# Moving a linear term, the eviction of a unit and the last group's PSUM banks in a woven four-layer kernel

## The chip, the cores and the metric

The kernel runs on one core of a Trainium2 chip, as one program in one launch. The metric is the device time of that core in microseconds (us); the runs of the kernel before have a median of 7454.95 us (three runs, 7451.15 to 7469.55). A core has a matrix engine (TensorE, PE in the profile; its weight loads are listed as PEld), VectorE (DVE), ScalarE (ACT), GpSimd (POOL) and SyncE (SP), which issues nearly all DMAs here. Each engine takes its own instructions strictly in order and waits for the others by semaphores. Matmuls write to PSUM, which has eight banks of 128 x 512 float32.

## The reference

The input is 16 images of 32 channels and 128 x 128 points, float32. Four layers follow, each added to its own input after a group normalisation `_gn`:

```python
x = x + _L0_conv_ref(_gn(x), ...)   # recurrent layer over 128 columns
x = x + _L1_conv_ref(_gn(x), ...)   # sum of absolute differences, 3x3
x = x + _L2_conv_ref(_gn(x), ...)   # 2-d Hartley transform, 32x32 modes mixed
x = x + _L3_conv_ref(_gn(x), ...)   # edge operators, small U-net, product
```

The second layer is the costly one. Input and weights are rounded to whole numbers of up to 127, and each output is

```python
out = -jnp.sum(jnp.abs(patches[None] - w[:, None]), axis=1)   # 32 channels x 9 taps
```

for 32 output channels, which no matrix product computes. The kernel uses |x - w| = 2 max(x - w, 0) - (x - w): the sum of max(x - w, 0) needs one element-wise pass per weight, the sum of x is a convolution with equal weights (the *linear term*), the sum of w is a constant. The fourth layer normalises the image, applies five fixed edge operators normalised over channels and rows, conv1 to conv4 with pooling, three transposed convolutions with conv5 to conv7, and multiplies its normalised input with the result.

## The kernel before, in words

**Stage 0** (`stage0`) is the recurrent layer. It isn't touched.

**The difference stage** (`Differences.run`, L608) walks over 16 images in two halves of 64 rows: 32 *units*. `q` holds one half, four copies of its 32 channels over the 128 partitions, one for each of four output channels that are computed at once. For each of 72 steps `i` (8 sets of four output channels x 9 taps) one pass writes max(q - w, 0) into a tile of 128 x 64 x 128 half-precision values: on DVE (L681, `d_dve`, three buffers) or on ACT (L678, `d_act`, two buffers). `sums` (L579) then adds the tile up over channels with 16 matmuls (L584) into the unit's four PSUM banks `acc1`. `linear` (L592, L600) adds the linear term, 9 taps x 16 matmuls; here it stands first, and its first tap has `start=True`, which clears the banks. `finish` (L563) evicts the unit before: four `scalar_tensor_tensor` (L567) from PSUM into the residual `xr`, then four `bn_stats` (L569). The four banks are used by one unit after the other, so nothing of the new unit can be summed before the old one is evicted. In the kernel before, `finish` is issued when three `d_dve` tiles of the new unit stand unsummed (L640), then comes the whole linear term, then the sums.

**The background.** The other two layers run in four *groups* of four images (`After.work`, L887): `forward` (transform, `mixing`), `back` (inverse transform and residual), `statistics` of the edge operators (L1263), `conv1`, `small_layers`, `last`. A group may start once its four images have left the difference stage; groups 0, 1 and 2 are one generator and follow each other. It is woven into the difference stage by a planner, `Weave` (L300), when the program is built. The planner keeps estimated times for PE, DVE and ACT. The background is a generator: a positive yield is PE time just issued, a negative one a time to let pass before the next step, `SUMMED` a wait for PE. `advance` (L384) lets steps out while PE is free ahead of the next sum. So the yields and the `weave.dve += ...` entries decide only where an instruction stands in its engine's order; they are no waits on the chip. `keep_order` fixes that order. The background has four PSUM banks (`b_ps`), the difference stage the other four.

**The drain** (`drain`, L403). After the last unit two generators run alternately by their planned times: what is left of groups 0 to 2 (`weave`), and group 3 (`end.weave`), which takes over the four banks of the difference stage (`c_ps`).

Places that the change touches in the background:

- `mixing` (L1082): 32 steps of 16 small matmuls; the weights come in eight tiles `mix` of 1 MB, in a ring of three. A new one is loaded once a tile has been used.
- `back` (L1117): 16 steps; `take_out` (L1171) adds two PSUM banks to the residual (L1176) and takes statistics (L1178). At the end `normalised` leaves mean and scale in `stats3`.
- `frames` (L1217): loads padded images of x3 and scales them on ACT (L1248); its first call makes `fr_shift` on DVE (L1245).
- `spread` (L1532): adds a bias and writes a layer's output on the engine it is told.
- `last` (L1659): four units of two rounds. A round sums conv7 into four banks (`up.round`, L808), then for each of four images `s` = bank x scale + 1 (L1730) and `multiply` (L1692): two strided `scalar_tensor_tensor` (L1695) of 256 values a partition. `done` (L1701) adds the mean on ACT (L1703), `store` writes 2 MB in four DMAs (L1709), `reload` loads the unit after next (L1673). A DMA covers 8 rows of all 32 channels of four images: 32 partitions, four runs of 4 KB each. The x1 tiles of the difference stage (`jc_rows`, L294: four row blocks x 32 channels over 128 partitions, one run of 4 KB each) have the other arrangement.

Of the kernel before, what the change touches and what calls it, by code (L numbers as in the profile page):

```python
# [299 lines left out]
class Weave:  # L300
# [10 lines left out]
    def __init__(self, work):  # L311
# [3 lines left out]
        self.draining = False  # L315
# [87 lines left out]
def drain(*weaves):  # L403
# [4 lines left out]
    while live:  # L408
        w = min(live, key=lambda w: w.now)
        us = w.step()  # L410
        w.now = max(w.now + (us or 0.0), w.until)
        w.due(float("inf") if us is None else w.now)
        if us is None:
            live.remove(w)

# [22 lines left out]
def rest(nc, tc, cst, sel16, bias, m1, r1, a, d, out):  # L438


    with ExitStack() as ctx:
# [13 lines left out]
        end.side, end.ps = "right", ctx.enter_context(tc.tile_pool(name="c_ps", bufs=4, space=PSUM))  # L455
        end.weave = Weave(end.work([NG - 1]))
# [5 lines left out]
class Differences:  # L462
# [100 lines left out]
    def finish(self, b, half, acc, xr):  # L563
# [4 lines left out]
        for k in range(4):  # L568
            nc.vector.bn_stats(self.stat[:, b, 4 * half + k, :], v[k])  # L569
        def store():  # L570
# [5 lines left out]
        self.weave.dve = max(self.weave.dve, self.weave.pe) + 5.6  # L576
        self.weave.later(max(self.weave.dve - self.weave.base, 0.0) + 0.5, store)

    def sums(self, acc, d, i, last):  # L579
        c = 1 if i % 3 == 1 else 0  # L580
        for k in range(4):
            for j in range(4):
# [5 lines left out]
                    start=False,  # L588
# [3 lines left out]
    def linear(self, acc, q):  # L592

        for tap in range(9):
            kh, kw = tap // 3, tap % 3
            for j in range(4):
                for k in range(4):
                    rows = slice(32 * k, 32 * k + 32)
                    row = 16 * j + 4 * k + kh
                    self.nc.tensor.matmul(  # L600
                        acc[k][32 * j : 32 * j + 32, :],
                        self.sel16[rows, 8, :],
                        q[rows, row : row + 4, kw : kw + W],
                        start=tap == 0,
                        stop=False,
                    )

    def run(self, tc, ctx, weave):  # L608
# [16 lines left out]
        for b in range(B):  # L625
            for half in range(2):
                q, acc = following, None
                late, xq = [], {}

                def sums(until, last):  # L630

                    while late and (min(late)[0] <= until or last):
                        end, n, act, t = min(late)
                        late.remove((end, n, act, t))
                        self.sums(acc, t, n, last and not late)
# [3 lines left out]
                for i in range(72):  # L639
                    if not acc and sum(not v[2] for v in late) == 3:  # L640

                        if before:
                            self.finish(*before)
                            weave.pe = max(weave.pe, weave.dve)
                        acc = [ps.tile([128, 512], F32, name="acc1") for _ in range(4)]
                        self.linear(acc, q)
                        weave.pe += 4.0
                        sums(weave.dve, False)
                    if i == 8 and (b, half) != (B - 1, 1):
# [38 lines left out]
                    else:  # L688
                        weave.advance(weave.dve + (3 - made) * DVE_US + (5.6 if before else 0.0))
# [1219 lines left out]
```

## Time and profile before

| what | value |
|---|---|
| runs, median of 3 | 7454.95 us (7451.15 to 7469.55) |
| profiled execution | 7434.2 us |
| its span, first to last instruction | 7432.4 us |
| mean granted TensorE clock | 0.86 |
| busy: PE / DVE / ACT | 5602.5 / 5881.6 / 5276.7 us |
| difference taps on ACT (L678) | 593 x 7146 ns |
| difference taps on DVE (L681) | 1711 x 2361 ns |
| linear term on PE (L600) | 4608 matmuls, 151.8 us |
| evictions (L567) | 128 x 745 ns |
| DMA | 721.68 MB, 31% of 16 engines' time |

A row of groups has the line, engine, operation and tile, the count, busy time and mean duration. A row of waits has the instruction that waited, what released it, the sum, the number of times and the longest. In a timeline each row is start, length, engine, line, operation, tile; the bracket holds the idle time of the engine before it and what ended it. In a table by stretches the numbers after the length are busy times of PE, PE weight load, DVE, ACT and POOL with counts, then the clock, the DMA share and GB/s. In the chain of waits PE has 14% of the span by steps that the trace can follow, most of it in the drain.

### The profile page before, as it was taken

How to read it: one execution, taken by the hardware profiler on the slowest of the kernel's cores; microseconds unless marked ns; L12 is line 12 of the kernel's file. 1: busy time of each engine (PE TensorE's matmuls, PEld its weight loads, DVE VectorE, ACT ScalarE, POOL GpSimd, SP SyncE). 2: the span in 40 equal slices, each digit the busy share in tenths (PEclk: the TensorE clock that was granted, in tenths of full speed). 3: DMA queues.
4: the chain of work that ended last, by engine and by line, in shares of the span. 5: the costliest groups of instructions: out<-in, count | busy, mean ns of one | idle time of the engine just before them, and what ended most of it. 6: DMA issues, size and time to landing. Idle time of an engine off the chain costs nothing. (4 is left out here: it accounts for less than half of the span.)

```text
span 7432.4 us, 258307 instructions
## 1 busy us (share of the span) xinstructions
PE 5602.5 (75%) x121132; PEld 3087.2 (42%) x121132; DVE 5881.6 (79%) x7180; ACT 5276.7 (71%) x3110; POOL 34.2 (0%) x31
## 2 busy tenths in 40 slices
PE   4888466666676777998777676998777775898897
PEld 3666232222244343333344343333335345554554
DVE  7787599999988989999898988998898994135223
ACT  2556398889987988898898888898887980122222
POOL 0000000000000000000000000000000000000000
PEclk9899788888878888999888887998888885897996
DMA  8655111111033333111433332221343234244314
GB/s 314 225 183 172 61 64 54 46 53 52 33 95 95 119 110 96 57 53 46 98 108 103 102 111 94 63 67 42 75 113 108 82 117 144 65 141 119 80 30 95
DMA packets 374270, 721.68 MB, mean 97 GB/s; under 512 B 50896, under 2 KB 219856, under 8 KB 362320
## 3 DMA queue, kind: packets, MB, share of 16 engines
q1 hardware_dynamic: 372768, 704.58, 31.0%
q8 instruction: 948, 15.53, 0.9%
q14 instruction: 122, 1.00, 0.0%
q10 hardware_dynamic: 432, 0.57, 0.0%
HBM read 507.21 MB, written 164.32 MB: 90 GB/s over the span
## 5 line engine op out<-in xcount | busy, mean ns | idle before, releaser
L678 ACT ACTIVATE d_act<-q,neg 128x8192 f16<-128x8192 f16 (+1 forms) x593 | 4199.2, 7146 | 559.1 <-PE acc L584 512.6
L681 DVE TENSOR_SCALAR d_dve<-q,qw 128x8192 f16<-128x8192 f16 (+1 forms) x1711 | 3941.9, 2361 | 348.3 <-PE acc L584 306.1
L584 PE MATMUL acc<-d_dve,sel 128*32 128x512 f16 x27376 | 1963.3, 416 | 747.7 <-DVE d_dve L681 734.5
L584 PEld LDWEIGHTS <-sel 128*32 128x32 f16 x36864 | 1078.8, 103 | 2405.6 <-issue 1816.9
L1603 PE MATMUL acc<-xp,wf 32*32 32x512 f32 x25600 | 1014.7, 620 | 30.6 <-issue 15.2
L584 PE MATMUL acc<-d_act,sel 128*32 128x512 f16 x9488 | 738.6, 438 | 256.1 <-ACT d_act L678 244.0
L1603 PEld LDWEIGHTS acc<-xp,wf 32*32 32x32 f32 x25600 | 443.5, 105 | 404.4 <-issue 299.4
L1542 ACT ACTIVATE y<-pooled,b 32x128 f32<-32x128 f32 x512 | 204.7, 400 | 519.2 <-DVE pooled L1528 510.4
L819 PE MATMUL acc<-y,u_conv 32*32 32x256 f32 (+1 forms) x9728 | 443.3, 515 | 87.4 <-DVE s L1730 39.5
L207 PE MATMUL pg<-h,wb 64*64 64x20 f32 (+15 forms) x4096 | 403.1, 324 | 95.3 <-DVE h L256 54.1
L207 PE MATMUL pg<-e,wb 64*64 64x20 f32 (+15 forms) x4096 | 360.4, 320 | 16.0 <-DVE e L260 4.3
L244 ACT ACTIVATE gt<-pg,bias 128x20 f32<-128x20 f32 (+15 forms) x1024 | 315.5, 374 | 78.1 <-PE pg L207 70.9
L1248 ACT ACTIVATE xp<-xp,fr_shift,stats 128x1280 f32<-128x1280 f32 (+1 forms) x128 | 182.8, 1434 | 230.1 <-DMA xp<-x_d 174.2
L207 PEld LDWEIGHTS pg<-h,wb 64*64 64x64 f32 x4096 | 251.1, 156 | 131.0 <-DVE h L256 80.7
L819 PEld LDWEIGHTS acc<-y,u_conv 32*32 32x32 f32 x9728 | 199.7, 119 | 252.0 <-issue 155.4
L207 PE MATMUL pg<-xn,wb 64*64 64x28 f32 (+61 forms) x4096 | 291.1, 308 | 10.7 <-ACT gt L244 3.3
L207 PEld LDWEIGHTS pg<-e,wb 64*64 64x64 f32 x4096 | 256.1, 158 | 94.0 <-DVE e L260 65.8
L600 PE MATMUL acc<-q,sel 32*32 32x512 f16 x4608 | 151.8, 532 | 148.1 <-DVE xr L567 99.1
L1703 ACT ACTIVATE xr<-xr,l_ms 128x1024 f32<-128x1024 f32 x64 | 69.9, 1140 | 267.1 <-DVE xr L1695 267.1
L255 ACT ACTIVATE th<-c 128x20 f32<-128x20 f32 (+15 forms) x256 | 81.3, 320 | 239.7 <-DVE c L253 238.2
L1288 PE MATMUL acc<-xp 32*64 32x204 f32 (+3 forms) x8576 | 233.2, 343 | 13.5 <-issue 13.5
L207 PEld LDWEIGHTS pg<-xn,wb 64*64 64x64 f32 x4096 | 222.5, 157 | 35.7 <-ACT gt L244 8.3
(203 smaller groups left out, 4215.5 us busy)
## 6 DMA issues: line engine op xcount, KB each, us to landing
xr<-x_d SPq DMA_DIRECT2D x192, 512.0 KB
xp<-x_d SPq DMA_DIRECT2D x112, 640.0 KB
q<-q_d SPq DMA_DIRECT2D x32, 2145.0 KB
x_d<-xr SPq DMA_DIRECT2D x128, 512.0 KB
x_in<-in_x_dram SPq DMA_DIRECT2D x16, 2048.0 KB
res<-in_x_dram SPq DMA_DIRECT2D x64, 512.0 KB
xn<-in_xs_dram SPq DMA_DIRECT2D x64, 512.0 KB
xn<-xn SPq DMA_DIRECT2D x128, 256.0 KB
```

Source lines behind the costliest of these rows:

```text
L207: nc.tensor.matmul(bank[c][q][64 * pair : 64 * pair + 64, :, :width], wb[half, 4 * kind + KIND[q]].rearrange("p b o -> p (b o)"), v[half], ...
L244: nc.scalar.activation(gt[:, q, :, :n], bank[c][q][:, :, :n], AF.Tanh if q == G else AF.Sigmoid, bias=bias[:, KIND[q] : KIND[q] + 1],)
L255: nc.scalar.activation(th[:, :, :n], cell, AF.Tanh)
L584: self.nc.tensor.matmul(acc[k][32 * j : 32 * j + 32, :], self.sel16[:, i // 9, :], d[:, row : row + 4, c : c + W], start=False, stop=last,)
L600: self.nc.tensor.matmul(acc[k][32 * j : 32 * j + 32, :], self.sel16[rows, 8, :], q[rows, row : row + 4, kw : kw + W], start=tap == 0, stop ...
L678: nc.scalar.activation(dst, src, AF.Relu, bias=self.neg[:, i : i + 1])
L681: nc.vector.tensor_scalar(dst, src, self.qw[:, i : i + 1], 0.0, ALU.subtract, ALU.max)
L819: nc.tensor.matmul(acc[blk][32 * j : 32 * j + 32, o : o + rows * n], t[part, 4 * par + tap, :], src[part, top : top + rows, left : left + ...
L1248: nc.scalar.activation(v, v, AF.Identity, bias=shift[0], scale=self.stats3[:, 1])
L1288: nc.tensor.matmul(gram[blk][j : j + width, at : at + n], xp[part, l, 2 + j : 2 + j + width], xp[part, rows, j : j + width + 4], start=sta ...
L1542: nc.scalar.activation(d, s, AF.Identity, bias=bj)
L1603: nc.tensor.matmul(acc[blk][32 * j : 32 * j + 32, :], tap_of("all", tap)[rows], xp[rows, 4 * j + kh : 4 * j + kh + 4, kw : kw + W], start= ...
```

## The change

The linear term no longer stands first. `linear` does one tap a call, called at every fourth step from 24 to 56; none of its matmuls starts the banks, and the first sum of a unit has `start=True` instead. The eviction is issued at two unsummed `d_dve` tiles, not three, and the planner counts 2.6 us for it before PE may go on, 5.6 for DVE.

In the background: `mixing` has places in its order for the weights (five of 5 us), `take_out` stands 4.5 instead of 7 us after its step, the shift of the frames is made at the end of `back`. In `last` the DMAs take one image each over all 128 partitions, `s` is written with its two column phases interleaved, and `multiply` is one contiguous instruction. When one of the drain's generators has ended, the other is `alone`: its `acc` takes banks from both pools by turns of four, `spread` uses DVE for even and ACT for odd images, and a store is planned 4 instead of 14 us after its unit.

```diff
 def drain(*weaves):
...
         if us is None:
             live.remove(w)
+            for w in live:
+                w.alone = True
...
         end.side, end.ps = "right", ctx.enter_context(tc.tile_pool(name="c_ps", bufs=4, space=PSUM))
+        end.spare = bg
...
-        self.weave.dve = max(self.weave.dve, self.weave.pe) + 5.6
+        start = max(self.weave.dve, self.weave.pe)
+        self.weave.pe, self.weave.dve = start + 2.6, start + 5.6
...
-    def sums(self, acc, d, i, last):
+    def sums(self, acc, d, i, first, last):
...
-                    start=False,
+                    start=first,
                     stop=last,
...
-    def linear(self, acc, q):
+    def linear(self, acc, q, tap):
-        for tap in range(9):
-            kh, kw = tap // 3, tap % 3
-            for j in range(4):
+        kh, kw = tap // 3, tap % 3
+        for j in range(4):
...
-                        start=tap == 0,
-                        stop=False,
+                    start=False,
+                    stop=False,
+        self.weave.pe = max(self.weave.pe, self.weave.now) + 0.45
...
-                        self.sums(acc, t, n, last and not late)
+                        self.sums(acc, t, n, not summed, last and not late)
+                        summed += 1
...
-                    if not acc and sum(not v[2] for v in late) == 3:
+                    if not acc and sum(not v[2] for v in late) == 2:
                         if before:
                             self.finish(*before)
-                            weave.pe = max(weave.pe, weave.dve)
                         acc = [ps.tile([128, 512], F32, name="acc1") for _ in range(4)]
-                        self.linear(acc, q)
-                        weave.pe += 4.0
                         sums(weave.dve, False)
+                    if i % 4 == 0 and 24 <= i < 60:
+                        self.linear(acc, q, i // 4 - 6)
...
-                        weave.advance(weave.dve + (3 - made) * DVE_US + (5.6 if before else 0.0))
+                        weave.advance(weave.dve + (2 - made) * DVE_US + (2.6 if before else 0.0))
...
     def acc(self):
-        return self.ps.tile([128, 512], F32, name="acc")
+        self.banks += 1
+        ps = self.spare if self.weave.alone and self.banks // 4 % 2 else self.ps
+        return ps.tile([128, 512], F32, name="acc")
...
-            yield 1.1
+            yield 1.0
+            if ky % 4 == 3 and 8 < ky < M1 - 1:
+                yield -5.0
...
                 if previous:
-                    yield -7.0
+                    yield -4.5
                     take_out(*previous)
...
             yield from normalised(nc, zp_, self.ps, weave, mv, 1, cst["avg2_bc"], 1e-5, self.stats3)
+            nc.vector.scalar_tensor_tensor(
+                self.shift3, self.stats3[:, 0], -1.0, self.stats3[:, 1], ALU.mult, ALU.mult
+            )
+            yield -2.5
...
-                if not shift:
-                    shift.append(pool.tile([128, 1], F32, name="fr_shift"))
-                    nc.vector.scalar_tensor_tensor(
-                        shift[0], self.stats3[:, 0], -1.0, self.stats3[:, 1], ALU.mult, ALU.mult
-                    )
-                nc.scalar.activation(v, v, AF.Identity, bias=shift[0], scale=self.stats3[:, 1])
+                nc.scalar.activation(v, v, AF.Identity, bias=self.shift3, scale=self.stats3[:, 1])
...
-            if engine is nc.vector:
+            if blk % 2 == 0 if weave.alone else engine is nc.vector:
...
-            def at(t, unit, j):
-                first = t.offset + g * 4 * CHW + (32 * unit + 8 * j) * W
-                return bass.AP(t.tensor, first, [[HW, 32], [CHW, 4], [1, 8 * W]])
+            def at(t, unit, blk):
+                first = t.offset + (4 * g + blk) * CHW + 32 * unit * W
+                return bass.AP(t.tensor, first, [[8 * W, 4], [HW, 32], [1, 8 * W]])
...
-                for j in range(4):
-                    nc.sync.dma_start(xr[32 * j : 32 * j + 32], at(self.d["x3"], unit, j))
+                for blk in range(4):
+                    nc.sync.dma_start(xr[:, blk], at(self.d["x3"], unit, blk))
...
-                for pc in range(2):
-                    v = x[:, blk].rearrange("p (r a w b) -> p r a w b", a=2, b=2, w=64)[:, :, pr, :, pc]
-                    nc.vector.scalar_tensor_tensor(v, v, mean[:, blk : blk + 1], s[:, pc], ALU.subtract, ALU.mult)
-                weave.dve += 1.0
+                v = x[:, blk].rearrange("p (r a w) -> p a r w", a=2, w=W)[:, pr]
+                nc.vector.scalar_tensor_tensor(
+                    v, v, mean[:, blk : blk + 1], s.rearrange("p r w b -> p r (w b)"), ALU.subtract, ALU.mult
+                )
+                weave.dve += 0.7
...
-                following[unit] = weave.later(14.0, lambda: store(x, unit))
+                following[unit] = weave.later(4.0 if weave.alone else 14.0, lambda: store(x, unit))
...
-                for j in range(4):
-                    nc.sync.dma_start(at(self.out, unit, j), x[32 * j : 32 * j + 32])
+                for blk in range(4):
+                    nc.sync.dma_start(at(self.out, unit, blk), x[:, blk])
...
-                        s = yp.tile([128, 2, 4, 64], F32, name="s", bufs=3)
+                        s = yp.tile([128, 4, 64, 2], F32, name="s", bufs=3)
                         nc.vector.tensor_scalar(
-                            s.rearrange("p b r w -> p (b r w)"),
-                            acc[blk],
+                            s.rearrange("p r w b -> p b r w"),
+                            acc[blk].rearrange("p (b r w) -> p b r w", b=2, w=64),
...
-            yield -36.0
+            yield -16.0
```

## The prediction

> **What bounds the kernel now.** I cut the span into its three stages with the table by stretches: the recurrent layer (to 920 us), the absolute-difference layer with the other layers woven into it (to 6132), and the drain, which finishes groups 2 and 3.
>
> ```profile
> 0.00:920.00 920.00, 623.16 (x12324) 483.55 (x12340) 674.75 (x2217) 432.54 (x1354) 2.42 (x7) 0.89 0.56 192
> 920.00:6132.00 5212.00, 3923.91 (x79680) 1915.34 (x79653) 4793.49 (x3912) 4573.59 (x1246) 26.92 (x16) 0.87 0.27 81
> 6132.00:7432.00 1300.00, 1055.41 (x29158) 688.28 (x29142) 413.31 (x1053) 270.60 (x512) 4.89 (x8) 0.80 0.36 96
> ```
>
> Columns after the length: PE, PE weight load, DVE, ACT, POOL busy, clock, DMA share, GB/s. In the middle stage DVE (92%) and ACT (88%) share the 2304 taps and set the time; PE has 1288 us free. In the drain PE (81%) sets it. The waits of the middle stage say what its two engines lack:
>
> ```profile
> ACT d_act L678 <- PE acc L584: 512.6, 68, 25.1
> DVE d_dve L681 <- PE acc L584: 306.1, 102, 18.5
> PEld acc L1092 <- DMA mix<-in_mix_dram: 57.1, 3, 21.6
> ACT xp L1248 <- DVE fr_shift L1245: 36.3, 2, 19.5
> ```
>
> Where they arise: the timeline at one change of unit (DVE, then ACT, then PE).
>
> ```profile
> 2066.01 2.72 DVE L567 SCALAR_TENSOR_TENSOR xr<-acc,sumw,xr 128x512 f32<-128x512 f32 x4
> 2068.65 2.46 DVE L569 BATCH_NORM_STATS2 stat<-xr 128x6 f32<-128x512 f32 x4
> 2074.76 6.88 DVE L681 TENSOR_SCALAR d_dve<-q,qw 128x8192 f16<-128x8192 f16 x3 [3.64 <-PE acc L584]
> ...
> 2073.94 7.23 ACT L678 ACTIVATE d_act<-q,neg 128x8320 f16<-128x8320 f16 x1 [6.23 <-PE acc L584]
> ...
> 2066.82 6.03 PE L600 MATMUL acc<-q,sel 32*32 32x512 f16 x144 [6.47 <-DVE xr L567]
> 2072.78 1.05 PE L584 MATMUL acc<-d_act,sel 128*32 128x512 f16 x16
> ```
>
> The new unit's tiles wait full while the old sums are evicted and the whole linear term (6.03 us) runs; only then does the first sum free a buffer. Adding up idle time from 10 us before to 20 us after each of the 32 evictions in the timeline, waits for sums cost DVE 164 and ACT 398 us.
>
> **Exchange rate.** A tap takes 2.361 us on DVE (L681) or 7.146 on ACT (L678), so of the joint rate DVE has 0.75 and ACT 0.25: a microsecond freed on DVE shortens this stage by 0.75, on ACT by 0.25.
>
> **Middle stage.**
> *Linear term, eviction after two tiles, first sum with start.* The eviction comes one tile (2.36) earlier, and ACT's sum follows the four evictions (2.72 + 0.5 = 3.2 after their start) instead of 2073.94 - 2066.01 = 7.9: 7.1 us earlier. ACT's waits of 5 to 25 us shrink by min(wait, 7), together 215. DVE has a third buffer free and bn_stats (2.46) to run, so its wait vanishes but for some 20: 145. Gain 0.75 x 145 + 0.25 x 215 = 163 (bounds 0 and 0.75 x 164 + 0.25 x 398 = 222). Queued behind the eviction on DVE is then only bn_stats and the third tile.
> *Nine linear pieces later in the unit.* The same 144 matmuls, 4.7 us a unit (151.8 / 32), hidden in PE's free time; without that cover, as in the three units from 2930 to 3400 us where PE is busy 452 of 470 and in group 1's like them, six units pay 28. I take +8, bounds 0 and 28.
> *Mixing, five places for the weights to land.* PE stood three times for them, and DVE and ACT behind it 51 and 44 (single gaps of 18.5, 15.4, 2.9, 14.3 and 15.8, 15.6, 13.0). All would be 0.75 x 51 + 0.25 x 44 = 49; I take 40, bounds 0 and 49.
> *shift3 earlier* frees at most 0.25 x 36 = 9; the frames must land too: 5. *Take-out 4.5 instead of 7, a store 4 instead of 14 after its unit, 16 instead of 36 at the end of `last`*: places in the queues of DVE and SP alone, 0; the matmuls that a take-out waits for stand a whole step ahead.
> *multiply*: 128 pieces of 0.49 become 64 of about 0.70 (L1176's 0.683, L567's 0.745): 18 us of DVE, 14. The interleaved write of s I take at its row's 0.81.
> *Work moved out.* A shorter stage holds less background. In the built order 24 take-outs (0.683 + 0.680), small statistics (8) and 8 frame scalings (15 us of ACT) of group 2 fall behind the last tap: 0.75 x 41 + 0.25 x 15 = 35 less here.
> Sum: -163 + 8 - 40 - 5 - 14 - 35 = -249.
>
> *The turned loads and stores of `last`.* Each is still 512 KB, but outermost in DRAM now stand 4 row blocks, not 32 channels; the pattern is the x1 loads' own (L560). Three stretches in which one kind runs (L560; old L1673; old L1709):
>
> ```profile
> 2493.00:2497.00 4.00, 2.67 (x28) 1.20 (x31) 4.00 (x3) 4.00 (x2) 0.00 (x0) 0.50 0.25 102
> 3564.00:3570.00 6.00, 5.29 (x62) 2.34 (x52) 3.02 (x4) 6.00 (x2) 0.00 (x0) 0.69 1.03 208
> 7424.00:7431.00 7.00, 0.00 (x0) 0.00 (x0) 0.00 (x0) 0.00 (x0) 0.00 (x0) 0.50 0.92 207
> ```
>
> The old form keeps all 16 DMA engines busy at 208 GB/s, the L560 form a quarter of them at 102. A group's 16 MB go from 81 to 164 us on four engines which also carry q, xq, xr1 and x2: 5.6 MB, 55 us, a unit. Group 0's `last` lasts 215 us (3550 to 3765): 164 + 74 = 238 of work, 23 too much, for each of two groups, on xq and xr3, which ACT and DVE wait for in order; SP stands too, since a reload waits for its store. +35; bounds 0 and 2 x 83.
>
> On this form the skill has two rules. The Trainium skill, "SBUF — State Buffer", Door 1: The DMA port swizzle, says that 32 partitions reach 8 of 16 ports and 128 all of them; by it alone the new form would be twice as fast and the last store about 5 us shorter. "DMA: Bandwidth & Descriptors", Why a DMA increments its semaphore by 16 and not by 1, says that a copy runs on the largest number up to 16 that divides both slowest dimensions: 16 before, 4 after. The 102 GB/s row sides with the second.
>
> **Drain.**
> *Group 2's rest*: 160 L1198 matmuls (19.4 us / 256 each) and 1344 L1288 (83.5 / 2848) are 12 + 39 = 51 us of PE. PE has 90 us free from 6132 to 6332, but the conv1 of group 2 that filled 6332 to 6432 (87% busy) starts later. +45, bounds 0 and 90.
> *Group 3's `last`*: from its first load (7286.5) to the end are 146 us. Eight transfers of 2 MB at 102 GB/s are 164, and 4 of start and landing: +22, bounds -10 (compute on eight banks) and +35.
> *Eight banks and two engines taking out*: in the built order only some 290 matmuls of group 3's conv1 follow group 2's last; what is left is 7182 to 7287, where the chain has about 30 us off PE between rounds. -15, bounds 0 and -30.
> Sum +52.
>
> **Forecast.** -249 + 35 + 52 = -162: the span goes from 7432.4 to 7270, the execution from 7434.2 to 7272. The runs' median, 7454.95, is 0.28% above that execution: 7272 x 1.0028 = **7292 us**. Own range 7220 to 7370.
>
> **Rivals.**
> *More gain*: the drain's first 200 us swallow group 2's rest and four engines suffice in the middle: 45 + 35 less, and 20 more by the bounds of the transition: 7190. For it, the 90 us of free PE; against it, PE at 94% of the clock and 92% busy right after.
> *Half the gain*: ACT's waits come from tiles made too far ahead, so they reappear elsewhere in the unit, and DVE's with them: +81, and the drain +45: 7420. For it: 25 us is the longest ACT wait, three times what the change removes at one place. Against: DVE's typical 3.6 to 5 us is all linear term.
> *Slower*: the four DMA engines. If none of the extra 83 us a group lies beside other work, two groups cost 166 instead of 35, group 2's `last`, which group 3's frames queue behind, 83 more, and the gain at the transitions is half: 7292 + 131 + 83 + 81 = 7587. It decides once stalls on xq, xr3 and frames pass 170 us. For it: one queue in order, and ACT already waits for xq eight times (40.6 us on the whole span). Against: 41 of the 164 us are loads issued well ahead.
> *The change doesn't do what it says*: eight banks come too late to matter: +15, inside the forecast's range.
>
> **How the numbers follow.** Forecast 0.70, more gain 0.12, half 0.10, slower 0.08. A measurement of this kernel tells about 0.3% from no change. Faster takes the first two and half of the third, 0.87; same 0.05; slower 0.08. Leaving out the slower rival and the tails of the others gives 7190 to 7400.
>
> **What would show it.** Right: no 6 us block of linear matmuls behind an eviction, DVE waits on L584 near 120 us, ACT's near 260; the last tap about 215 us sooner; the drain 1340 to 1360 us; the DMA share near 0.25 in the last 20 us. Wrong: ACT or DVE waiting over 100 us for xq or xr3; DVE's sum waits above 230; a drain over 1420.

## The result and the profile after

| what | before | after |
|---|---|---|
| runs, median | 7459.88 us (7451.15 to 7469.55, 4 runs) | 7327.97 us (7323.21 to 7330.26, 4 runs) |
| ratio, with its 95% interval | | 0.9822 [0.9805, 0.9839] |
| profiled execution, span | 7432.4 us | 7321.4 us |
| first to last difference tap ("stage") | 5208.9 us | 5079.2 us |
| from the last tap to the end ("drain") | 1303.8 us | 1325.8 us |
| DVE / ACT busy in the stage | 4791 / 4573 us | 4735 / 4588 us |

The change takes 1.8% off the time. The profiled executions are single ones: that of the kernel before lies 0.3% under its median and that of the kernel after 0.06%, so the spans show 111 us of gain where the medians show 132. Some 20 us between two spans, stages or drains can be scatter of this kind. Stage and drain are cut in the trace at the first start and the last end of a tap on DVE. The table by stretches of the kernel after (after the length: busy PE, PE weight load, DVE, ACT, POOL, then clock, DMA share, GB/s):

```profile
0.00:914.00 914.00, 618.55 (x12308) 475.02 (x12309) 673.68 (x2216) 432.43 (x1353) 2.42 (x7) 0.91 0.56 193
914.00:5998.00 5084.00, 3852.55 (x78064) 1807.07 (x78064) 4736.87 (x3737) 4588.05 (x1211) 30.35 (x15) 0.87 0.24 78
5998.00:7321.40 1323.40, 1018.23 (x30762) 696.11 (x30760) 447.28 (x1078) 296.14 (x568) 5.10 (x9) 0.81 0.37 112
```

DVE is now busy for 93% of the stage and ACT for 90%, so these two still set it. The third row is 23 us longer than before's although the program's layers are the same: the shorter stage holds less of the background, and what it doesn't hold falls behind the last tap (30762 matmuls in the row, 29158 before).

The same change of unit that the forecast showed, in the timeline (start, length, engine, line; DVE, then ACT, then PE):

```profile
1903.69 2.72 DVE L570 SCALAR_TENSOR_TENSOR xr<-acc,sumw,xr 128x512 f32<-128x512 f32 x4
1906.33 2.46 DVE L572 BATCH_NORM_STATS2 stat<-xr 128x6 f32<-128x512 f32 x4
1908.71 27.42 DVE L687 TENSOR_SCALAR d_dve<-q,qw 128x8320 f16<-128x8320 f16 x12
...
1907.19 28.17 ACT L684 ACTIVATE d_act<-q,neg 128x8192 f16<-128x8192 f16 x4 [1.85 <-PE acc L589]
...
1904.49 2.59 PE L589 MATMUL acc<-d_act,sel 128*32 128x512 f16 x16 [4.17 <-DVE xr L570]
```

The 6 us block of linear matmuls is gone. PE adds the first tile up while the four evictions still run (one bank after the other, 2.59 us for the 16 matmuls), ACT stands for 1.85 us instead of 6.23, and DVE goes from `bn_stats` straight into twelve taps. The waits of the stage (instruction, releaser; sum in us, times, longest):

```profile
ACT d_act L684 <- PE acc L589: 320.3, 53, 22.2
DVE d_dve L687 <- PE acc L589: 146.9, 85, 28.6
ACT xq L537 <- DMA xq<-x_d: 77.1, 6, 27.3
DVE xr L1705 <- DMA xr<-x_d: 47.1, 8, 18.8
DVE xm L1011 <- DMA xm_d<-xm: 23.6, 1, 23.6
DVE xr L1189 <- DMA xr<-x_d: 22.9, 1, 22.9
```

Against 512.6 and 306.1 before, the waits for sums fell by 192 on ACT and 159 on DVE. The other four rows are new or larger: before, ACT waited 25.7 us for xq, DVE 12.2 us for `back`'s residual, and not at all for the two others. All four are transfers. With the smaller rows, DVE waits 144 us of the stage for transfers and ACT 111, where it was 37 and 39 before. One of their places, in the timeline of DVE, then ACT, during group 0's `last`:

```profile
3707.46 0.75 DVE L1705 SCALAR_TENSOR_TENSOR xr<-xr,l_ms,s 128x512 f32<-128x512 f32 x1 [18.79 <-DMA xr<-x_d]
...
3722.21 0.75 DVE L1705 SCALAR_TENSOR_TENSOR xr<-xr,l_ms,s 128x512 f32<-128x512 f32 x1 [4.24 <-DMA xr<-x_d]
...
3727.23 1.24 ACT L537 ACTIVATE xq<-xq,shift,r 128x1024 f32<-128x1024 f32 x1 [27.27 <-DMA xq<-x_d]
```

`multiply` waits for one reloaded image after the other, and the x1 tile that ACT needs next, on the same queue, comes 27 us late. Just ahead of this a store of `last`, a load of q and an x1 tile are on their way together:

```profile
3640.00:3690.00 50.00, 42.69 (x1028) 19.35 (x1020) 48.67 (x34) 50.00 (x12) 0.00 (x0) 0.90 0.26 105
```

One kind alone has a DMA share of 0.25, and the three together have no more (0.28 at most in any 10 us of this stretch): they share the same quarter of the DMA engines.

**How gains and stalls are counted below.** A microsecond of idle or busy time taken from DVE is worth 0.75 us of the stage and one from ACT 0.25, as in the forecast. Experiments ran in several sessions, in which the kernel before had medians of 7444 to 7460 us. So a difference between kernels of different sessions is taken from their ratios to the kernel before, times 7455 us, with the profiled spans beside it where useful.

### The profile page after: what moved, and what is told of

It reads as the page before. It is cut to its first block, busy times and chain, and to the rows that moved or that the text cites. A ratio compares the mean times of both kernels' runs of the same rounds, so it can differ in the third digit from the quotient of the medians.

```text
span 7321.4 us, 258237 instructions
## 1 busy us (share of the span) xinstructions
PE 5489.3 (75%) x121132; PEld 2978.2 (41%) x121132; DVE 5857.8 (80%) x7030; ACT 5316.6 (73%) x3132; POOL 37.9 (1%) x31
## 5 line engine op out<-in xcount | busy, mean ns | idle before, releaser
L589 PEld LDWEIGHTS <-sel 128*32 128x32 f16 x36864 | 1051.7, 103 | 2559.0 <-issue 1907.3
L1614 PE MATMUL acc<-xp,wf 32*32 32x512 f32 x25600 | 1033.6, 617 | 43.0 <-DVE pooled L1539 13.9
L589 PE MATMUL acc<-d_act,sel 128*32 128x512 f16 x9584 | 759.5, 439 | 395.4 <-ACT d_act L684 325.1
L1614 PEld LDWEIGHTS acc<-xp,wf 32*32 32x32 f32 x25600 | 411.1, 104 | 409.6 <-issue 312.5
L1259 ACT ACTIVATE xp<-xp,shift,stats 128x1280 f32<-128x1280 f32 (+1 forms) x128 | 182.6, 1434 | 514.9 <-DMA xp<-x_d 372.9
L825 PE MATMUL acc<-y,u_conv 32*32 32x256 f32 (+1 forms) x9728 | 349.5, 460 | 102.3 <-DVE s L1742 67.0
L825 PEld LDWEIGHTS acc<-y,u_conv 32*32 32x32 f32 x9728 | 171.1, 110 | 223.9 <-issue 134.2
L1299 PEld LDWEIGHTS acc<-xp 32*64 32x64 f32 (+1 forms) x8576 | 174.7, 138 | 126.6 <-issue 92.6
L1705 DVE SCALAR_TENSOR_TENSOR xr<-xr,l_ms,s 128x512 f32<-128x512 f32 x128 | 94.5, 760 | 114.4 <-DMA xr<-x_d 114.4
```

Source lines behind the costliest of these rows:

```text
L589: self.nc.tensor.matmul(acc[k][32 * j : 32 * j + 32, :], self.sel16[:, i // 9, :], d[:, row : row + 4, c : c + W], start=first, stop=last,)
L825: nc.tensor.matmul(acc[blk][32 * j : 32 * j + 32, o : o + rows * n], t[part, 4 * par + tap, :], src[part, top : top + rows, left : left + ...
L1259: nc.scalar.activation(v, v, AF.Identity, bias=self.shift3, scale=self.stats3[:, 1])
L1299: nc.tensor.matmul(gram[blk][j : j + width, at : at + n], xp[part, l, 2 + j : 2 + j + width], xp[part, rows, j : j + width + 4], start=sta ...
L1614: nc.tensor.matmul(acc[blk][32 * j : 32 * j + 32, :], tap_of("all", tap)[rows], xp[rows, 4 * j + kh : 4 * j + kh + 4, kw : kw + W], start= ...
L1705: nc.vector.scalar_tensor_tensor(v, v, mean[:, blk : blk + 1], s.rearrange("p r w b -> p r (w b)"), ALU.subtract, ALU.mult)
```

## The experiments

**The difference stage's part alone (e3).** The kernel before, with only this of the change (shown in extracts; the first sum's start and the planner's times for the eviction belong to it):

```diff
-                        start=tap == 0,
+                    start=False,
...
-                    if not acc and sum(not v[2] for v in late) == 3:
+                    if not acc and sum(not v[2] for v in late) == 2:
...
+                    if i % 4 == 0 and 24 <= i < 60:
+                        self.linear(acc, q, i // 4 - 6)
```

> The kernel before with the change of the difference stage alone: linear term in nine pieces later in the unit, first sum with start, eviction at two tiles, the planner's times for it. Theory (the term of the sum, 163 us less on the middle stage, part of which the drain gives back): 7310 to 7350, waits for sums around the evictions 30 us or less on DVE. Rival (ACT's waits go elsewhere in the unit): 7370 to 7420.

Measured: 7317.83 us (7301.58 to 7323.8), ratio 0.9823 [0.9809, 0.9838]. That is the ratio of the whole change, and it lies in the theory's band; around the evictions DVE waits 14 us for sums, as the theory had it too. Its stretches, and its waits in the stage:

```profile
919.00:5874.00 4955.00, 3814.59 (x76922) 1774.62 (x76925) 4719.50 (x3771) 4604.48 (x1213) 38.57 (x15) 0.89 0.26 79
5874.00:7299.00 1425.00, 1094.26 (x31909) 764.90 (x31898) 466.55 (x1186) 295.40 (x552) 5.07 (x9) 0.79 0.39 108
```

```profile
ACT d_act L681 <- PE acc L586: 233.9, 47, 16.8
DVE d_dve L684 <- PE acc L586: 159.5, 88, 18.7
```

The stage is 254 us shorter than before, and the drain 121 longer: at the last tap 4288 matmuls of the last two groups' statistics and 512 of their `back` are left, where before had 2944 and 256 (a group has 2144 and 256, so all of group 2's are left here). Nearly half of what the stage gains is given back there. All the other parts together, DMAs included, bring the whole change nothing more than this one part.

**Its two halves, put back one at a time (e8, e6).** e8 is the kernel after with the whole linear term in front of the sums again and the eviction left at two tiles:

```diff
-                    start=False,
+                    start=tap == 0,
...
                         acc = [ps.tile([128, 512], F32, name="acc1") for _ in range(4)]
+                        for t in range(9):
+                            self.linear(acc, q, t)
                         sums(weave.dve, False)
-                    if i % 4 == 0 and 24 <= i < 60:
-                        self.linear(acc, q, i // 4 - 6)
```

> The changed kernel with the linear term whole and first again (it starts the banks), the eviction still after two tiles. Theory (the linear term delays the first sums by 4.7 us for ACT and lets DVE wait some 2.3 us a unit): the middle stage 70 to 110 us longer than 5079, of which the drain takes back up to a half; 7370 to 7420. Rival (PE has the time, so its place doesn't matter): below 7350.

Measured: 7383.12 us (7364.99 to 7390.29), ratio 0.9904 [0.9874, 0.9935]: 61 us more than the changed kernel by the ratios, as the theory had it. Its stage is 5186.8 us, 108 longer than after's, and its drain 1280.7, 45 shorter. A change of unit in its timeline:

```profile
1915.94 2.72 DVE L570 SCALAR_TENSOR_TENSOR xr<-acc,sumw,xr 128x512 f32<-128x512 f32 x4
1916.74 6.04 PE L604 MATMUL acc<-q,sel 32*32 32x512 f16 x144 [3.29 <-DVE xr L570]
...
1924.69 14.24 ACT L684 ACTIVATE d_act<-q,neg 128x8192 f16<-128x8192 f16 x2 [13.83 <-PE acc L589]
1926.37 9.18 DVE L687 TENSOR_SCALAR d_dve<-q,qw 128x8192 f16<-128x8192 f16 x4 [3.04 <-PE acc L589]
```

The block is back, and both engines stand behind it. Around all 32 evictions (from 10 us before each to 20 us after) ACT waits 321 us for sums and DVE 55, against 203 and 25 in the kernel after and 398 and 165 before. e6 puts back the other half:

```diff
-                    if not acc and sum(not v[2] for v in late) == 2:
+                    if not acc and sum(not v[2] for v in late) == 3:
...
-                        weave.advance(weave.dve + (2 - made) * DVE_US + (2.6 if before else 0.0))
+                        weave.advance(weave.dve + (3 - made) * DVE_US + (2.6 if before else 0.0))
```

> The changed kernel with the eviction after three unsummed tiles of DVE, not two; the linear term stays late in the unit. Theory (the linear term ahead of the sums is the larger part; the third tile costs only ACT, 2.4 us a unit at the rate of 0.25): 7335 to 7355, DVE's waits for sums around the evictions under 40 us. Rival (the place of the eviction is the larger part): 7390 or more.

Measured: 7358.74 us (7348.52 to 7366.36), ratio 0.9874 [0.9846, 0.9903], 39 us more than the kernel after by the ratios, just above the theory's band and well short of the rival's. Its stage is 69 us longer than after's and its drain 28 shorter; around the evictions ACT waits 265 us for sums and DVE 37. So the linear block was the dearer half (108 against 69 us of the stage), and the third tile counts as well, for DVE too and not for ACT only.

**The old DMAs in the changed kernel, and the new ones in the old (e1, e2).** e1 is the kernel after with the loads and stores of `last` as before; e2 is the kernel before with the reverse of this edit:

```diff
-            def at(t, unit, blk):
-                first = t.offset + (4 * g + blk) * CHW + 32 * unit * W
-                return bass.AP(t.tensor, first, [[8 * W, 4], [HW, 32], [1, 8 * W]])
+            def at(t, unit, j):
+                first = t.offset + g * 4 * CHW + (32 * unit + 8 * j) * W
+                return bass.AP(t.tensor, first, [[HW, 32], [CHW, 4], [1, 8 * W]])
...
-                    nc.sync.dma_start(xr[:, blk], at(self.d["x3"], unit, blk))
+                    nc.sync.dma_start(xr[32 * j : 32 * j + 32], at(self.d["x3"], unit, j))
...
-                    nc.sync.dma_start(at(self.out, unit, blk), x[:, blk])
+                    nc.sync.dma_start(at(self.out, unit, j), x[32 * j : 32 * j + 32])
```

> The changed kernel with the loads and stores of `last` in their old arrangement (32 channels outermost, 32 partitions a DMA); all else as changed. Theory (the new arrangement runs on four DMA engines, which the difference stage needs too): 60 to 110 us faster than the changed kernel's 7328, so 7220 to 7270; in the difference stage ACT's waits for xq fall from 77 to under 40 us, DVE's for xr3 from 47 to under 10, and the last tap comes 40 to 70 us before 5998. Rival (the waits come from the order, which asks for xq and xr3 too early, whatever the DMAs look like): 7310 to 7340 and waits for xq and xr3 together still above 90 us.

> The kernel before with nothing but the new arrangement of those loads and stores. Theory of the four engines: 60 to 110 us slower than before, 7515 to 7570, with DVE waiting for xr3 and ACT for xq by over 80 us more in all. Rival (the order before has room enough for the slower transfers): 7445 to 7475.

Measured: e1 7264.98 us (7263.07 to 7265.71), ratio 0.9755 [0.9741, 0.977], in the theory's band; e2 7455.87 us (7439.66 to 7467.54, 10 runs) beside 7451.65 of the kernel before, ratio 1.0012 [1.0001, 1.0022]. In the changed kernel the turned DMAs cost 50 us by the ratios and 60 by the spans; in the kernel before 9 us by the ratios, nearly nothing, as the rival to the theory had it. Waits for transfers in the stage of e1, and then of e2:

```profile
DVE xr L1189 <- DMA xr<-x_d: 21.8, 1, 21.8
...
ACT xq L537 <- DMA xq<-x_d: 13.3, 3, 7.6
DVE xr L1705 <- DMA xr<-x_d: 6.4, 1, 6.4
```

```profile
ACT xq L534 <- DMA xq<-x_d: 29.4, 4, 9.5
...
DVE xr L1176 <- DMA xr<-x_d: 14.3, 1, 14.3
```

With the old form ACT waits 64 us less for xq and DVE 42 less for residuals: 0.25 x 64 + 0.75 x 42 = 48, and the stage is 46 us shorter. The drain is 17 us shorter, but that is a net: from the last conv1 matmul of group 3 to the end e1 takes 192 us and the kernel after 239, and ahead of it the drain of e1 is 30 us longer. In e2 the waits hardly differ from before's. The last stretch of the kernel after shows the form itself:

```profile
7300.00:7319.00 19.00, 0.00 (x0) 0.00 (x0) 0.00 (x0) 0.00 (x0) 0.00 (x0) 0.50 0.26 105
```

Nothing but stores runs, at 105 GB/s and a quarter of the DMA engines' time; before's last stretch had 207 GB/s at 0.92.

**Why the same DMAs cost so differently (e9 pair, e12).** In the traces, the multiplications of `last` of groups 0 and 1 fill units 17 and 27 of the kernel before (units counted from 0), and from 60 us ahead of them to their end ACT takes one x1 tile (`xq`) for each group. In the kernel after they have moved half a unit and a whole unit on, to stretches with two and four such tiles. The e9 pair holds `last` of group 0 back, in the kernel after and in e1:

```diff
         with self.pool("l_y") as yp, self.pool("l_x", 2) as xp:
+            if g == 0:
+                yield -190.0
```

> The changed kernel with a pause of 190 planned us ahead of group 0's `last`, so that in the built order the stores and reloads of both groups' `last` in the difference stage fall into second halves or the last image, where no xq is loaded. To be compared with e9_late_old_dma alone, which is the same with the old arrangement. Theory (the new form costs the middle stage 46 us because `last` now meets the xq loads on four engines, which it did not in the kernel before): the middle stages of the two differ by under 15 us, ACT's waits for xq are under 40 us in both. Rival (in the tighter schedule the slower transfers cost as much anywhere): 35 us or more.

> As e9_late_new_dma, with the old arrangement of the loads and stores of `last`. Theory: its middle stage is less than 15 us shorter than e9_late_new_dma's, its run 25 to 60 us shorter, by the closing part of the drain. Rival: its middle stage is 35 us or more shorter.

Measured: 7336.53 us (7333.03 to 7352.55), 0.9857 [0.9839, 0.9876], with the new form, and 7274.99 us (7255.76 to 7283.48), 0.9767 [0.9746, 0.9787], with the old: 62 us apart by the medians and 67 by the spans, at least as far as without the delay (60 by the spans). But their stages are only 27 us apart, which lies between what the theory and the rival expected. Waits in the stage, first with the new form, then with the old:

```profile
ACT xq L537 <- DMA xq<-x_d: 37.6, 4, 19.2
DVE xr L1707 <- DMA xr<-x_d: 16.1, 5, 4.2
```

```profile
ACT xq L537 <- DMA xq<-x_d: 23.2, 3, 11.6
```

ACT's waits for xq shrank below 40 us as the theory said, but the drain, 1432.9 against 1395.2 us, now lost 38 us where it had lost 17; what moves the loss there was not traced. e12 asks from the other side: e3 with the new form of the DMAs (the reverse of e1's edit), the rest of the background as before.

> The kernel before with the difference-stage part of the change (e3: ratio 0.9823, 7317.8 us, middle stage 4955, drain 1425) and, besides, the turned loads and stores of `last`; the rest of the background as before. Theory: the turned DMAs are dear wherever the linear part has taken the idle time at the changes of unit away and has moved `last` next to the x1 loads, whatever else of the background is changed: middle stage 35 to 60 us longer than e3's (4990 to 5015), waits of ACT on xq and of DVE on xr3 together above 60 us in it, drain 15 to 45 longer, ratio 0.989 to 0.997 (some 7370 to 7425 us). Rival: in the changed kernel they are dear only together with the other background parts (mixing's places, take-outs earlier, shorter waits to the stores), so here as cheap as in the kernel before: middle stage within 15 us of e3's, ratio 0.982 to 0.986 (up to 7345 us).

Measured: 7370.77 us (7359.37 to 7380.61), ratio 0.9899 [0.9869, 0.9929], 57 us more than e3 by the ratios, as the theory had it (the stage alone is 1 us above its band). Its stage is 61 us longer than e3's and its drain 19, with these waits in the stage, where e3 had 9.0 and 10.6:

```profile
ACT xq L534 <- DMA xq<-x_d: 57.6, 6, 15.9
...
DVE xr L1698 <- DMA xr<-x_d: 32.7, 10, 4.1
```

By the rates above, these two waits make 0.25 x 49 + 0.75 x 22 = 29 of the 61 us. The rest is idle time of other names: in all DVE is idle for 59 us more in the stage than in e3, ACT for 61.

| pair, old form to new | x1 tiles beside the two `last` (new) | stage | drain |
|---|---|---|---|
| before, e2 | 2 | -8 | +31 |
| e9 old, e9 new | 1 | +27 | +38 |
| e1, after | 6 | +46 | +17 |
| e3, e12 | 6 | +61 | +19 |

The linear part alone is enough to make the turned DMAs dear. Stage and drain are single profiles here: the rows add up to 23, 65, 63 and 80 us, where the ratios give 9, 67, 50 and 57. The pairs with most x1 loads beside `last` lose most in the stage, which fits the neighbourhood as a cause and does not prove it. The second row, with the fewest loads, still loses 27 us, so the neighbourhood isn't the whole of it; that the idle time at the changes of unit had covered the rest in the kernel before fits the first row, but no run tried it by itself.

**What the rest of the background does.** e3 and e1, both with the old DMAs, differ in all other parts of the change. By the ratios these gain 51 us, but in an unexpected way: e1's stage is 78 us *longer* than e3's and its drain 117 shorter. With the new DMAs (e12 and the kernel after) it is 63 longer and 118 shorter. In the stage DVE waits 95 us for transfers in e1 and 20 in e3, ACT 47 and 39: 0.75 x 75 + 0.25 x 8 = 58 of the 78. At the last tap e1 has 1120 matmuls fewer to do than e3, all of them group 2's `back`: a piece of the background has moved from the drain into the stage, where it stands for transfers. Two of the parts are taken out one at a time below (e4, e5); the earlier take-outs, the pauses, `shift3` and `multiply` were not.

**Nobody told that it is alone (e4).**

```diff
         if us is None:
             live.remove(w)
-            for w in live:
-                w.alone = True
```

> The changed kernel in which no generator is ever told that it is alone: four banks to the end, each layer's output taken out on the engine it is told, stores planned 14 us after their unit. Theory (eight banks and two engines give 15 us): 7335 to 7355. Rival (they come too late, and the closing part is bound by four DMA engines): 7320 to 7335.

Measured: 7364.07 us (7346.75 to 7369.27), ratio 0.9884 [0.9867, 0.9901]: 46 us more by the ratios, 39 by the spans, above the theory's band and further above the rival's. The stage is the same (5082.4), the drain 31 us longer. From the last conv1 matmul of group 3 to the end it takes 271 us, in the kernel after 239: the eight banks, the two engines and the earlier stores, which go together here, are worth some 32 us there.

**The old mixing (e5).**

```diff
-            yield 1.0
-            if ky % 4 == 3 and 8 < ky < M1 - 1:
-                yield -5.0
+            yield 1.1
```

> The changed kernel with the mixing as before: a planned 1.1 us a step and no places for the weights. Theory (the term of 40 us in the sum): 7350 to 7375, with DVE and ACT standing behind PE three times for the weights by 13 to 19 us each. Rival (the time that the order sets aside is missing elsewhere): 7315 to 7345.

Measured: 7382.03 us (7380.09 to 7392.5), ratio 0.9911 [0.9878, 0.9945], 66 us more by the ratios: more than the theory and far more than the rival. But not where either had put it: the stage is 5070.5 us, 9 *shorter* than after's, though PE stood twice for mix weights in it, 30 us in all, and the drain is 1387.4, 62 longer. The first 400 us of the drain, in e5 and then in the kernel after:

```profile
5991.00:6191.00 200.00, 140.81 (x1677) 131.42 (x1677) 90.64 (x213) 17.91 (x31) 3.60 (x2) 0.56 0.65 200
6191.00:6391.00 200.00, 137.38 (x3804) 114.13 (x3804) 84.73 (x178) 17.97 (x32) 0.67 (x3) 0.54 0.57 174
```

```profile
5996.00:6196.00 200.00, 151.32 (x2202) 139.66 (x2194) 83.87 (x207) 22.98 (x40) 3.81 (x3) 0.61 0.66 198
6196.00:6396.00 200.00, 137.15 (x4766) 99.94 (x4760) 88.91 (x184) 22.29 (x45) 0.42 (x2) 0.70 0.51 155
```

e5 does 5481 matmuls there and the kernel after 6968, at a clock of 0.54 to 0.56 against 0.61 to 0.70. The 1487 that are missing are 53 us of work at the 28 matmuls per us of the next 200 us (5617). So the loss arises at the entrance of the drain. PE is busy for nearly as long there in both (278 and 288 us); its matmuls last longer in e5, those of the statistics 472 ns on average in the second of these stretches, against 408 in the kernel after. Why the old order goes with a lower clock there, no run took apart.

**The other transfers on four engines (e10, e11).** Both start from e1. e10 loads each q as four DMAs of 32 partitions, with the channels outermost; e11 does the same for the x1 loads and x2 stores of the difference stage as well:

```diff
-        self.nc.sync.dma_start(q, bass.AP(q_d.tensor, first, [[0, 4], [(H + 2) * P, C], [1, (self.R + 2) * P]]))
+        for o in range(4):
+            part = bass.AP(q_d.tensor, first, [[(H + 2) * P, C], [1, (self.R + 2) * P]])
+            self.nc.sync.dma_start(q[32 * o : 32 * o + 32].rearrange("p r w -> p (r w)"), part)
```

```diff
-    return bass.AP(t.tensor, first, [[16 * W, 4], [HW, C], [1, rows * W]])
+    for j in range(4):
+        ap = bass.AP(t.tensor, first + 16 * W * j, [[HW, C], [1, rows * W]])
+        v = sb[32 * j : 32 * j + 32]
+        nc.sync.dma_start(ap if store else v, v if store else ap)
```

> The kernel of e1_old_dma, with each load of q made as four DMAs of 32 partitions, channels outermost, instead of one DMA with the four copies outermost. Theory (q is the largest transfer on the four busy engines, and the stage begins by waiting 40 us for it): 7235 to 7255, the first wait for q near 30 us. Rival (all but the first load is hidden anyway): 7256 to 7272.

> The kernel of e10_q_sixteen with the x1 loads (xq, xr1) and the x2 stores of the difference stage made as four DMAs of 32 partitions each too, so that no large transfer is left on four engines alone. Theory (the four engines were what was left of the DMA waits): 7185 to 7203. Rival (with q gone from them they have room, and SP issues four times as many DMAs): 7200 to 7230.

Measured: e10 7202.55 us (7195.33 to 7203.48), ratio 0.9664 [0.9636, 0.9691]; e11 7162.7 us (7162.57 to 7164.22), ratio 0.962 [0.9602, 0.9637]. Both gain more than any theory gave them, and e11 beats both kernels of the case. While the first q is loaded, the stretches of the kernel after and of e10 are:

```profile
890.00:906.00 16.00, 0.00 (x0) 0.00 (x0) 0.00 (x0) 0.00 (x0) 0.00 (x0) 0.50 0.25 69
```

```profile
882.00:890.00 8.00, 0.00 (x0) 0.00 (x0) 0.00 (x0) 0.00 (x0) 0.00 (x0) 0.50 0.92 209
```

The load in e10 keeps 0.92 of the DMA engines' time busy instead of 0.25 and moves three times as much per microsecond, so the first tap starts at 896.4 instead of 919.6 in e1. The stage is 41 us shorter besides. The transfer waits left in e10's stage:

```profile
DVE xw L1077 <- DMA xw<-xm_d: 12.6, 5, 4.0
ACT xp L1261 <- DMA xp<-x_d: 10.9, 2, 9.8
ACT xq L537 <- DMA xq<-x_d: 4.5, 2, 2.4
...
DVE xm L1013 <- DMA xm_d<-xm: 3.9, 1, 3.9
```

In e1 DVE waited 66 us for xr, xm and xw and ACT 47 for xp and xq; here it is 17 and 15. 0.75 x 49 + 0.25 x 32 = 45, as much as the whole gain of the stage. The transfers waited for are not q: it was the load of q that had made them late. e11 takes 34 us more off the stage (4957.3 us) and 6 off its start; DVE's idle time in the stage falls by 34 us, 25 of them waits for transfers, and ACT's by 34, 14 of them for transfers: 0.75 x 34 + 0.25 x 34 = 34, all of it.

The Trainium skill, "DMA: Bandwidth & Descriptors", Why a DMA increments its semaphore by 16 and not by 1, says that a DMA runs on the largest number up to 16 which divides the slowest dimension of both its sides; 4 copies give 4 engines, 32 channels give 16. The shares of 0.25 and 0.92 above agree.

## Why the prediction was right, step by step

- **The sum.** Forecast 7292 us in a range of 7190 to 7400; measured 7328. The forecast change is -162; measured is -132 by the medians and -111 by the spans. By the ratios it splits into three parts: the difference stage's -132 (e3), forecast -163 + 8 - 35 + 45 = -145; the other background's -51 (e1 against e3), forecast -40 - 5 - 14 - 15 = -74; the turned DMAs' +50 (the kernel after against e1), forecast +57. So each part is right in sign and near in size. Where the time goes is not: in the stage and the drain the first part has -254 and +121 (forecast -190 and +45), the second +78 and -117 (forecast -59 and -15). These errors pull opposite ways, so that the stage (-130 for -214) and the drain (+22 for +52) came out nearer than their parts is luck.
- **The changes of unit** were sized well. Around the evictions the waits for sums fell from 164 to 25 us on DVE (145 forecast as gain, 139 measured) and from 398 to 203 on ACT (215 and 195): 0.75 x 139 + 0.25 x 195 = 153, against 163. e8 and e6 show that both the block and the third tile were in it. What is left on ACT has single longer waits in it, 14.16 us at 1201 us for one, where ACT has run ahead of the old unit's last sums.
- **Mixing, -40 in the stage: the step that failed in its place.** The three stops of PE for weights have shrunk to one of 3 us in the stage. Yet with the old mixing (e5) the stage is 9 us shorter, not 40 longer. The gain is there all the same, 62 us, at the head of the drain, a place that the forecast did not name.
- **The turned DMAs, +35 in the stage and +22 for the end.** Together 57 forecast, 50 measured by the ratios and 60 by the spans of after and e1, as 46 and 17 (the first tap makes up the rest). The 17 for 22 is luck: the closing 47 us, from 192 to 239, are twice the forecast, and the drain ahead of them is 30 shorter. The mechanism was right, transfers on four engines making xq and xr3 late. But it was applied to these DMAs alone: in e1, with the old form, DVE still waits 95 us for transfers in the stage, where it was 37 before, and e10 frees most of that by turning q. No term of the sum had this. That they would cost the same in any kernel was silently assumed, and e2 showed it wrong: in the kernel before they cost 0.12% [0.01%, 0.22%].
- **Work moved out and group 2's rest, 35 and 45.** The kernel after has just the 160 and 1344 matmuls more behind the last tap that the forecast counted. The exchange is right in kind and was under-sized for the linear part alone, which in e3 moves the stage by -254 and the drain by +121. In the whole change the drain keeps only +22, since the other background parts give 117 back, with mixing (62) and the lone generator (32) in it. The earlier take-outs and shorter pauses, put at nothing because they are places in queues alone, may have a share in this and in the longer stage; no run tells.
- **Eight banks and two engines, -15.** Measured -32 in the drain and -46 by the ratios (e4), with the earlier stores in it: too small by a factor of two to three.
- **`multiply`, 0.70 us a piece.** Measured 0.760 us over 128 pieces, 4 us for the 64 in the stage. DVE's busy time in the stage fell by 56 us where the forecast's rows made it 59 (18 of `multiply` and 41 of moved work). Part of this nearness is luck: summed row by row, `multiply` fell by 15 and the take-outs by 33, and six taps of together 15 us went from DVE to ACT, which the forecast did not have.
- **What would show it.** The block is gone, DVE's waits for sums are 147 us (forecast 120) and ACT's 320 (260), the DMA share at the end is 0.26. The last tap came 133 us sooner, not 215, and the drain is 1326 us, below the 1340 to 1360 that were named. Waits for xr3 at L1705 reach 114 us over the whole span, beyond the 100 that the forecast gave as a sign against itself; 67 of them lie in the drain, so the sign was drawn too tight.
- **The rivals.** Half the gain (7420) and slower (7587) did not come: in the stage ACT and DVE waited 158 us for xq, xr3 and frames (77, 47 and 34), not far below the 170 from which the slower rival was to decide. More gain (7190) did not come either; it needed four engines to suffice in the middle, and they didn't. That eight banks come too late is refuted by e4.

## What to carry to other kernels

When two engines share a stage, turn every wait into the stage's time by the share that each engine does, and expect a shorter stage to push interleaved work out behind it: here 121 of 254 us came back in the drain. Other parts of a change can pull work the other way, out of the tail into the stage: here these gave 117 us of the drain back and made the stage 78 us longer. Price a transfer by what else needs its DMA engines and its queue at that moment, not by its own wait: the same turned DMAs cost almost nothing before and some 50 us after, and turning q the other way paid mostly through transfers that were not q. Look at the DMA share while only one transfer runs: a quarter, as here with 4 outermost, calls for trying another outermost dimension; with 32 the share was 0.92.

## What the runs showed of the hardware that was not expected

- Four DMAs of 32 partitions with 32 channels outermost move a q of 2145 KB at 209 GB/s, one DMA of 128 partitions with four copies outermost at 69 to 73, with a DMA share of 0.92 against 0.25. Transfers of the second kind share one quarter of the engines: a store of `last`, a load of q and an x1 tile together had a share of 0.26. Issuing four times as many DMAs for q (e10) and then for x1 and x2 too (e11) cost nothing that shows: 68 us and another 33 us were gained by the ratios.
- The granted clock in the first 400 us of the drain was 0.54 to 0.56 in e5 and 0.61 to 0.70 in the kernel after, with PE busy for 278 and 288 of the 400 us.
- PE began to sum a unit into its first bank 0.80 us after the start of the four evictions, with the other three still to be read: 16 matmuls took 2.59 us there, and 1.05 us in the row of the kernel before.
